# A graph layer on one core: every 32nd quad's rows fetched singly, 32 indices to a register load, a chunk's edge scalars in one transfer

## The chip, the cores and the metric

The kernel runs on one core of one Trainium2 chip. The metric is device microseconds of that core; the time before is the median of three runs, 3920.53 us (3918.47 to 3926.07). A core has five instruction queues that run beside each other and meet at semaphores: TensorE (PE, matrix products), VectorE (DVE), ScalarE (ACT), GpSimd (POOL) and SyncE (SP, which only issues transfers). ACT and POOL issue transfers too.

## What is computed

One message-passing layer over 12,500 nodes with 160 features each (64 scalars and 32 three-vectors) and 400,000 edges that are sorted by destination, then a residual and a layer norm. Cut to what matters:

```
h_s = s @ lin1_ws * a / 8            # node table: 64 scalars
h_v = v @ lin1_wv * a / sqrt(32)     #             and 32 vectors of 3
hid = silu(edge_scalars @ fc_w1 / 8) # 64 scalars an edge
w   = hid @ fc_w2 / 8                # 224 weights an edge: w1..w5
es, ev = h_s[edge_src], h_v[edge_src]
m_s1 = w1 * es * e0                  # messages from weights, gathered rows
m_s2 = w4 * (ev . e1) / 3            # and the edge's four attributes e0, e1
m_v1, m_v2, m_v3 = (w2 * es) e1, w3 * ev * e0, w5 * cross(ev, e1) / 2
agg = segment_sum(messages, edge_dst) / 4
out = layernorm(x + gate(self_connection(x) + lin2(agg)))
```

## The kernel before

**Tables and tiles.** A short first stage writes the node table `h_tab` (12,500 rows of 640 bytes) to device memory. The edges then go in 3125 tiles of 128. Three tiles are a block (`BT`), twelve tiles a side (`SIDE`), two sides a chunk of 24 tiles (`CT`). A step of the main loop (L898) handles a quad: two tiles of each side, so that a chunk is six steps and the loop has 782 of them.

**A step.** `gather` (L468) fetches the quad's 512 rows of `h_tab`: one indirect transfer for each tile, four in all, issued by POOL into one of four buffers `hg`. `weights` (L526) multiplies the hidden layer by `fc_w2` on PE into `pw`. `products` (L538) multiplies `pw` by the gathered rows on DVE into `pr`. `one_hot` and `select_quad` make, on DVE, the matrices by which `add_tile` (L611) sums `pr` into the rows of a block on PE, two steps later (L944). `close` copies a finished pair of blocks out of PSUM (`sa`, ACT, L818); `turned` transposes it on PE and copies it on ACT (`tt`, L625 and L627); `second` applies the output maps on PE (L637) and copies on ACT (`os`, L640); `add` adds it to the accumulator on DVE (L645). `hide` (L776) makes the hidden layer of four tiles of each side at once, two steps ahead: a product of `w1` with the chunk's edge scalars `es` on PE (L463), and a Silu on ACT (L465). The hidden layer, the transposes, the maps and the finishing steps share two PSUM banks (`misc`) in turn. Every 30 steps a piece of the self connection is added, and as destinations are complete, `finish` (L648) norms and stores the nodes.

**Edge scalars.** `load_chunk` (L195) loads a chunk's scalars, in device memory a matrix of 64 rows by 400,000 edges, eight steps ahead (`LEAD`) on SP's queue: the first side to partitions 0 to 63 and the second to 64 to 127, 384 KB each, two transfers. `w1` has `fc_w1` twice on its diagonal, one block for each side. The last, short chunk has sides of three and two tiles.

**Singly fetched quads.** The list `own` (L477) names quads that POOL doesn't gather: every `OWN`-th from step `OWN` + 6, ending four steps before the last. Their rows come as 512 transfers of 640 bytes each, from addresses held in registers. `places` loads the quad's indices as four rows of `at_bytes`, `OWN` + 8 steps ahead; `fetch_rows` (L764) scales them to bytes on DVE, `OWN` + 1 steps ahead, and `rows_of` (L494) cuts them into batches of `BATCH` indices. A batch belongs to SP or to ACT: one instruction loads its indices into registers (L501), and then each of its rows is one transfer (L508) on that queue. `some_rows` (L516) issues the transfers by turns, SP then ACT (`TURNS`); it is called in four places of a step with the counts of `SLOTS`, so the issues stand between the other instructions of both queues. Whatever is left two steps before the quad's own would be an error (L773).

**Order.** The order of each queue is the order of the program (`manual_schedule`). Transfers of SP and ACT take their semaphores from one ring of eight: in the built program an issue waits for the landing of the transfer that used its place before, whichever queue issued that one.

Of the kernel before, what the change touches and what calls it, by code (L numbers as in the profile page):

```python
# [10 lines left out]
F32 = mybir.dt.float32  # L11
# [4 lines left out]
AF = mybir.ActivationFunctionType  # L16
# [5 lines left out]
P = 128  # L22
S = 64
# [11 lines left out]
SIDE = KB * BT  # L35
CT = 2 * SIDE
AHEAD = 3 * CT
NF = 4
OWN = 40
BATCH = 16  # L40
TURNS = "SA"
SLOTS = (4, 3, 4, 3)
LEAD = 8

MARGIN = 128
# [15 lines left out]
def gnn_kernel(  # L61
# [21 lines left out]
    nc = tc.nc  # L83
# [10 lines left out]
    consts = ctx.enter_context(tc.tile_pool(name="consts", bufs=1))  # L94
# [71 lines left out]
    def index(t):  # L166
        a0, idx, _ = ahead(t)
        return idx[:, t - a0:t - a0 + 1]
# [23 lines left out]

    ess = {}

    def load_chunk(c, queue=nc.sync):  # L195
        if c in ess:
            return
        t0, halves = chunks[c]
        es = ess[c] = loads.tile([2 * S, SIDE * P], F32, name="es")
        for half, n in enumerate(halves):  # L200
            to = es[half * S:(half + 1) * S]
            e0 = (t0 + half * halves[0]) * P
            queue.dma_start(to[:, :n * P], es_t[:, e0:e0 + n * P])


    ident = consts.tile([P, P], F32, name="ident")
# [3 lines left out]
    eps = consts.tile([P, 1], F32, name="eps")  # L210
    nc.vector.memset(eps, 1e-5)

    w1 = consts.tile([2 * S, 2 * S], F32, name="w1")
    nc.vector.memset(w1, 0.0)

    w2 = consts.tile([2 * S, 2, NWT], F32, name="w2")
    nc.vector.memset(w2, 0.0)
# [13 lines left out]
    with tc.tile_pool(name="nodes", bufs=len(starts)) as nodes, tc.tile_pool(  # L231
        name="nodes_ps", bufs=6, space=PSUM
# [19 lines left out]
        def spread(w, ap):  # L252

            return bass.AP(tensor=w.tensor, offset=w.offset, ap=[*ap, [1, w.shape[1]]])
# [63 lines left out]
            return m  # L318

        index(0)  # L320
        raw = ends_pool.tile([2 * S, NWT], F32, name="raw")
        for half in range(2):
            r = slice(half * S, (half + 1) * S)
            nc.sync.dma_start(w1[r, r], fc_w1)
            nc.sync.dma_start(raw[r], fc_w2)

        def bases():
# [51 lines left out]
    nc.vector.tensor_scalar_mul(half_at, at, 0.5)  # L379
    iota = consts.tile([P, W], F32, name="iota")  # L380
    nc.vector.tensor_copy(iota, iota_i)
    for half in range(2):
        r = slice(half * S, (half + 1) * S)
        at_c = 0
        for a, b in ((64, 128), (0, 64), (192, 224), (160, 192), (128, 160)):
            nc.vector.tensor_scalar_mul(w2[r, half, at_c:at_c + b - a], raw[r, a:b], 1.0 / math.sqrt(64))
            at_c += b - a
# [66 lines left out]
    def hidden(pool, psum, es, halves, t0, n):  # L454

        ph = psum.tile([2 * S, Q * P], F32, name="ph", tag="misc")
        hid = pool.tile([2 * S, Q * P], F32, name="hid")
        ends = [max(0, min(n, m - t0)) for m in halves]
        assert ends[0] >= ends[1]
        for k, c0, c1 in ((2 * S, 0, ends[1]), (S, ends[1], ends[0])):  # L460
            if c1 > c0:
                c = slice(c0 * P, c1 * P)
                nc.tensor.matmul(ph[:k, c], w1[:k, :k], es[:k, t0 * P + c0 * P:t0 * P + c1 * P],  # L463
                                 start=True, stop=True)
                nc.scalar.activation(hid[:k, c], ph[:k, c], AF.Silu, scale=1.0 / math.sqrt(64))  # L465
        return hid

    def gather(pool, idx):  # L468
# [249 lines left out]
    with tc.tile_pool(  # L718
# [271 lines left out]
        with tc.For_i(0, n_redo, 1):  # L990
# [9 lines left out]
            with tc.For_i(0, n_again, 1) as g, tc.For_i(0, GT, 1) as k:  # L1000
                t = g * GT + k
                idx = loads.tile([P, 1], I32, name="idx1", bufs=1)
                nc.sync.dma_start(idx, src[ds(g, 1), :, ds(k, 1)].rearrange("o p t -> p (o t)"))
                eat = loads.tile([P, 4], F32, name="eat1", bufs=1)
                nc.sync.dma_start(eat, ea[ds(g, 1), :, ds(k, 1)].rearrange("o p t k -> p (o t k)"))
                base0 = loads.tile([P, 1], I32, name="base1", bufs=1)
                nc.sync.dma_start(base0, of_tile[0:1, ds(t, 1)].to_broadcast([P, 1]))
                to = loads.tile([P, 1], I32, name="to1", bufs=1)
                nc.sync.dma_start(to, dst[:, ds(t, 1)])
                line = loads.tile([1, P], I32, name="line1", bufs=1)  # L1010
                with nc.allow_non_contiguous_dma(reason="one tile's destinations"):
                    nc.sync.dma_start(line, dst[:, ds(t, 1)].rearrange("p o -> o p"))
                ends = loads.tile([1, 2], I32, name="ends1", bufs=1)
                for k, op in enumerate((OP.min, OP.max)):
                    nc.vector.tensor_reduce(ends[:, k:k + 1], line, AX.X, op)
                nc.sync.dma_start(least, ends[:, 0:1])
                low = loads.tile([P, 1], I32, name="low1", bufs=1)
                nc.sync.dma_start(low, least.to_broadcast([P, 1]))
                es = loads.tile([2 * S, SIDE * P], F32, name="es")
                nc.sync.dma_start(es[:S, :P], es_t[:, ds(t * P, P)])  # L1020
                hid = hidden(edge, misc_ps, es, (1, 0), 0, 1)
                hg = gather(deep, [idx])
                pr = products(edge, weights(pw_ps, hid, [(0, 0)]), hg, 1)
                r = edge.tile([P, 1], F32, name="r", bufs=1)
                had = edge.tile([P, 2], F32, name="had", bufs=1)
                nc.vector.tensor_tensor(r, to, base0, op=OP.subtract)
                nc.vector.tensor_scalar(had[:, 0:1], r, 0.0, None, op0=OP.is_ge)
                nc.vector.tensor_scalar(had[:, 1:2], r, float(W), float(2 * NP), op0=OP.is_lt,
                                        op1=OP.mult)
                nc.vector.tensor_mul(had[:, 0:1], had[:, 0:1], had[:, 1:2])  # L1030
                nc.vector.tensor_tensor(r, to, low, op=OP.subtract)
                nc.vector.tensor_add(r, r, had[:, 0:1])
                first = nc.values_load(ends[0:1, 0:1], min_val=0, max_val=N - 1)
                last = nc.values_load(ends[0:1, 1:2], min_val=0, max_val=N - 1)
                with tc.For_i(first, last + 1, W) as base:
                    base = nc.s_assert_within(
                        base, 0, N - 1, skip_runtime_bounds_check_because="it is at most `last`")
                    pa = pa_ps.tile([P, 512], F32, name="pa")
                    sel = select(late, r, eat)
                    add_tile(pa, 0, sel, 0, pr[:, 0], start=True, stop=True)  # L1040
                    sa = late.tile([P, NPR], F32, name="sa")
                    nc.scalar.copy(sa[:ROWS], pa[:ROWS, :NPR])
                    tt = late.tile([P, 8, NO, W], F32, name="tt", bufs=1)
                    turned(misc_ps, sa, tt, 0, 1)
                    add(base, second(late, misc_ps, tt, 1), 0)
                    nc.vector.tensor_scalar_add(r, r, -float(W))
# [52 lines left out]
```

## Time and profile before

| | |
|---|---|
| time, median of 3 runs | 3920.53 us (3918.47 to 3926.07) |
| profiled execution: its time, its span | 3915.52 us, 3913.8 us |
| granted TensorE clock, mean | 0.972 |
| PE, matmuls: busy, share | 3634.4 us, 93% |
| DVE | 2441.2 us, 62% |
| ACT | 895.3 us, 23% |
| POOL | 2915.6 us, 74% |
| transfers | 413.16 MB, 106 GB/s over the span |
| single row fetches | 4864 on SP, 4864 on ACT |
| gathers on POOL | 3049 |

The profile is of one execution, taken by the hardware profiler. Busy time counts the work of an engine, not what its sequencer does: transfers that SP or ACT issue, register loads and waits are not in it. In rows of groups, "L472 POOL" is line 472 of the kernel on GpSimd; the names are the tile written, an arrow, and the tiles read; "x3049" is how often; then follow the busy time, the mean duration in ns, the idle time of the engine just before these instructions, and what ended most of it ("issue" is nothing that the profile shows). In rows of waits, "ACT sa L818 <- PE pa L613" is ScalarE idle before line 818 until TensorE's line 613 was done, with us in total, times, and the longest. Rows of the order in time begin with the start and the duration in us. "ACTq" is a queue's own instruction.

### The profile page before, as it was taken

Reading aid. Unit: us, or ns where it says so; the run is one execution under the profiler, and the core shown is the slowest. Engines: PE = TensorE matmul, PEld = TensorE weight load, DVE = VectorE, ACT = ScalarE, POOL = GpSimd, SP = SyncE. Lnnn points to the kernel's source line nnn. Section 1 sums busy time; section 2 is a strip of 40 time slices with the busy share of each in tenths; the row PEclk is TensorE's granted clock in tenths of the full one; section 3 lists DMA queues with packets and bytes.
Section 4 is the critical chain, followed back from the end, with each engine's and each line's share of the span. In section 5 each row is a group of like instructions: output and inputs, shape, how many; then the busy total and the mean of one; then the engine's idle time right before and its main releaser. Section 6 shows DMA issues by size and latency. Waiting matters only on the chain. (4 is left out here: it accounts for less than half of the span.)

```text
span 3913.8 us, 66881 instructions
## 1 busy us (share of the span) xinstructions
PE 3634.4 (93%) x14293; PEld 1589.8 (41%) x14293; DVE 2441.2 (62%) x6532; ACT 895.3 (23%) x2481; POOL 2915.6 (74%) x3096
## 2 busy tenths in 40 slices
PE   6899999999989999899899999989999999989998
PEld 4344344344334444344344343434444344334443
DVE  6656566666655666656566666656666665656655
ACT  2222222222222222222222222222222222222222
POOL 6777777777777777777777777777777777777774
PEclk8999999999999999999999999999999999999999
DMA  7344444444344443443444444444343443444432
GB/s 241 97 104 104 101 105 101 101 105 105 101 105 103 105 108 99 104 109 98 103 106 103 101 109 101 102 103 107 101 111 98 101 112 98 102 103 100 104 99 65
DMA packets 258055, 413.16 MB, mean 106 GB/s; under 512 B 92568, under 2 KB 186273, under 8 KB 257509
## 3 DMA queue, kind: packets, MB, share of 16 engines
q0 software_dynamic: 149312, 260.41, 25.7%
q1 hardware_dynamic: 98004, 145.13, 15.1%
q10 hardware_dynamic: 10322, 3.26, 0.4%
q14 instruction: 302, 2.47, 0.2%
q8 instruction: 115, 1.88, 0.2%
HBM read 392.53 MB, written 16.00 MB: 104 GB/s over the span
## 5 line engine op out<-in xcount | busy, mean ns | idle before, releaser
L472 POOL DMA_INDIRECT hg<-h_tab,idx x3049 | 2885.1, 946 | 942.6 <-issue 834.8
L534 PE MATMUL pw<-w,hid 128*128 128x448 f32 x3126 | 1346.2, 554 | 29.3 <-ACT hid L465 10.8
L613 PE MATMUL pa<-pr,sel 128*64 128x416 f32 x6250 | 1287.4, 533 | 0.2 <-ACT sa L818 0.2
L552 DVE TENSOR_TENSOR pr<-pw,hg 128x384 f32<-128x384 f32 x2289 | 1125.7, 547 | 0.0
L597 DVE TENSOR_TENSOR pw<-rel,iota 128x64 f32<-128x64 int16 x782 | 181.4, 232 | 956.4 <-PE pw L534 953.4
L534 PEld LDWEIGHTS pw<-w,hid 128*128 128x128 f32 x3126 | 553.5, 193 | 487.4 <-issue 420.3
L544 DVE TENSOR_TENSOR pr<-pw,hg 128x512 f32<-128x512 f32 x763 | 527.1, 691 | 346.3 <-DMA hg<-h_tab,idx 250.9
L613 PEld LDWEIGHTS pa<-pr,sel 128*64 128x64 f32 x6250 | 384.4, 138 | 799.0 <-issue 772.9
L818 ACT COPY sa<-pa 128x416 f32<-128x416 f32 x521 | 262.8, 505 | 1081.3 <-DMA hq<-h_tab 612.7
L463 PE MATMUL misc<-es,w 128*128 128x512 f32 (+1 forms) x784 | 446.2, 651 | 20.3 <-DVE rel L425 17.7
L465 ACT ACTIVATE hid<-misc 128x512 f32<-128x512 f32 x392 | 233.5, 596 | 784.0 <-DMA hq<-h_tab 379.3
L622 PEld LDWEIGHTS misc<-ident,sa 128*128 128x128 f32 x2084 | 242.8, 143 | 383.9 <-issue 254.9
L622 PE MATMUL misc<-ident,sa 128*128 128x128 f32 x2084 | 334.1, 284 | 69.2 <-ACT hid L465 56.6
L637 PE MATMUL misc<-tt,l 128*96 128x256 f32 (+5 forms) x1496 | 360.7, 390 | 32.9 <-DVE y L683 26.9
L606 DVE TENSOR_TENSOR sel<-pw,eas 128x256 f32<-128x256 f32 x782 | 324.3, 415 | 9.5 <-ACT eas L580 9.3
L637 PEld LDWEIGHTS misc<-tt,l 128*96 128x96 f32 (+1 forms) x1496 | 233.8, 168 | 179.1 <-issue 98.3
L625 ACT COPY tt<-misc 128x192 f32<-128x192 f32 x521 | 164.6, 316 | 559.8 <-DMA hq<-h_tab 371.4
L463 PEld LDWEIGHTS misc<-es,w 128*128 128x128 f32 x784 | 118.4, 190 | 282.9 <-issue 229.8
L645 DVE TENSOR_TENSOR acc<-acc,os 96x32 f32 x1042 | 195.6, 188 | 25.3 <-ACT os L640 6.8
L627 ACT COPY tt<-misc 128x64 f32<-128x64 f32 x521 | 117.1, 225 | 0.0
L670 PE MATMUL misc<-ident,acc 96*128 96x96 f32 x196 | 35.5, 266 | 77.2 <-DVE pw L597 46.4
L640 ACT COPY os<-misc 96x512 f32<-96x512 f32 (+2 forms) x68 | 38.3, 563 | 208.6 <-PE misc L637 202.3
(89 smaller groups left out, 672.8 us busy)
## 6 DMA issues: line engine op xcount, KB each, us to landing
es<-in_es_t_dram SPq DMA_DIRECT2D x258, 384.0 KB
hq<-h_tab SPq DMA_DIRECT2D x4864, 0.6 KB
hq<-h_tab ACTq DMA_DIRECT2D x4864, 0.6 KB
hg<-h_tab,idx POOLq DMA_INDIRECT x3049
h_tab<-ht POOLq DMA_DIRECT2D x24, 320.0 KB
xt<-in_x_dram SPq DMA_DIRECT2D x23, 320.0 KB
out_dram<-y SPq DMA_DIRECT2D x23, 320.0 KB
xv<-in_xv_t_dram SPq DMA_DIRECT2D x25, 187.5 KB
```

Source lines behind the costliest of these rows:

```text
L463: nc.tensor.matmul(ph[:k, c], w1[:k, :k], es[:k, t0 * P + c0 * P:t0 * P + c1 * P], start=True, stop=True)
L465: nc.scalar.activation(hid[:k, c], ph[:k, c], AF.Silu, scale=1.0 / math.sqrt(64))
L472: nc.gpsimd.indirect_dma_start(out=hg[:, t, :], out_offset=None, in_=h_tab, in_offset=bass.IndirectOffsetOnAxis(ap=i, axis=0))
L534: nc.tensor.matmul(pw[:, t:t + m, :NWT], hid[:m * S, c * P:(c + 1) * P], w2[:m * S, :m], start=True, stop=True)
L544: nc.vector.tensor_mul(two, pw[:, :n, :2 * S].rearrange("p t (k c) -> p t k c", k=2), hg[:, :n, None, :S].to_broadcast([P, n, 2, S]))
L552: nc.vector.tensor_mul(pr[:, :n, first:first + V3].rearrange("p t (i c) -> p t i c", i=3), pw[:, :n, None, 2 * S + k * V:2 * S + (k + 1) * ...
L606: nc.vector.tensor_mul(sel[:, :n], oh[:, :, None, :].to_broadcast([P, n, 4, W]), by_slot(tiles[0][0])[:, u:u + n, :, None].to_broadcast([P ...
L613: nc.tensor.matmul(pa[half * ROWS:(half + 1) * ROWS, :NPR], sel[:, t].rearrange("p k w -> p (k w)"), pr, start=start, stop=stop)
L622: nc.tensor.transpose(pt[:, four * P:four * P + k], sa[:k, c:c + P], ident[:k, :k])
L637: nc.tensor.matmul(po[:, k, :nb], l2[r, terms[to, part, four]], a[:, :nb], start=(n == 0), stop=(n == len(of) - 1))
L645: nc.vector.tensor_add(window, window, os[:, :, b])
L818: nc.scalar.copy(sa, pas.pop(j)[:, :NPR])
```

## The change

Three constants change: `OWN` from 40 to 32, `BATCH` from 16 to 32, `SLOTS` from (4, 3, 4, 3), 14 a step, to (5, 4, 4, 4), 17 a step. `load_chunk` loads a whole chunk by one transfer: row r of side h goes to partition 2 r + h. The short chunk keeps two transfers, to every second partition, after a memset. `w1` follows: `fc_w1` is loaded once with each of its rows on two partitions (`raw1`), and a product on DVE with `halves`, which holds 1/8 on the even or on the odd partitions, makes `w1`. The factor 1/8 before the Silu goes from the activation into `w1`. Lines of the changed kernel stand up to twelve further down.

```diff
@@ -36,10 +36,10 @@
 CT = 2 * SIDE
 AHEAD = 3 * CT
 NF = 4
-OWN = 40
-BATCH = 16
+OWN = 32
+BATCH = 32
 TURNS = "SA"
-SLOTS = (4, 3, 4, 3)
+SLOTS = (5, 4, 4, 4)
 LEAD = 8
 
 MARGIN = 128
@@ -192,15 +192,24 @@
 
     ess = {}
 
+    def side_of(es, half):
+
+        return es.rearrange("(r h) e -> h r e", h=2)[half]
+
     def load_chunk(c, queue=nc.sync):
         if c in ess:
             return
         t0, halves = chunks[c]
         es = ess[c] = loads.tile([2 * S, SIDE * P], F32, name="es")
+        if halves == (SIDE, SIDE):
+            of = es_t[0:1, t0 * P:t0 * P + 1]
+            queue.dma_start(es, bass.AP(tensor=of.tensor, offset=of.offset,
+                                        ap=[[es_t.shape[1], S], [SIDE * P, 2], [1, SIDE * P]]))
+            return
+        nc.vector.memset(es[:, :max(halves) * P], 0.0)
         for half, n in enumerate(halves):
-            to = es[half * S:(half + 1) * S]
             e0 = (t0 + half * halves[0]) * P
-            queue.dma_start(to[:, :n * P], es_t[:, e0:e0 + n * P])
+            queue.dma_start(side_of(es, half)[:, :n * P], es_t[:, e0:e0 + n * P])
 
 
     ident = consts.tile([P, P], F32, name="ident")
@@ -210,8 +219,7 @@
     eps = consts.tile([P, 1], F32, name="eps")
     nc.vector.memset(eps, 1e-5)
 
-    w1 = consts.tile([2 * S, 2 * S], F32, name="w1")
-    nc.vector.memset(w1, 0.0)
+    w1 = consts.tile([2 * S, 2, S], F32, name="w1")
 
     w2 = consts.tile([2 * S, 2, NWT], F32, name="w2")
     nc.vector.memset(w2, 0.0)
@@ -318,10 +326,11 @@
             return m
 
         index(0)
+        raw1 = ends_pool.tile([2 * S, S], F32, name="raw1")
+        nc.sync.dma_start(raw1, spread(fc_w1, [[S, S], [0, 2]]))
         raw = ends_pool.tile([2 * S, NWT], F32, name="raw")
         for half in range(2):
             r = slice(half * S, (half + 1) * S)
-            nc.sync.dma_start(w1[r, r], fc_w1)
             nc.sync.dma_start(raw[r], fc_w2)
 
         def bases():
@@ -379,6 +388,8 @@
     nc.vector.tensor_scalar_mul(half_at, at, 0.5)
     iota = consts.tile([P, W], F32, name="iota")
     nc.vector.tensor_copy(iota, iota_i)
+    nc.vector.tensor_mul(w1, raw1[:, None, :].to_broadcast([2 * S, 2, S]),
+                         halves[:, :, None].to_broadcast([2 * S, 2, S]))
     for half in range(2):
         r = slice(half * S, (half + 1) * S)
         at_c = 0
@@ -460,9 +471,9 @@
         for k, c0, c1 in ((2 * S, 0, ends[1]), (S, ends[1], ends[0])):
             if c1 > c0:
                 c = slice(c0 * P, c1 * P)
-                nc.tensor.matmul(ph[:k, c], w1[:k, :k], es[:k, t0 * P + c0 * P:t0 * P + c1 * P],
-                                 start=True, stop=True)
-                nc.scalar.activation(hid[:k, c], ph[:k, c], AF.Silu, scale=1.0 / math.sqrt(64))
+                nc.tensor.matmul(ph[:k, c], w1.rearrange("p h c -> p (h c)")[:, :k],
+                                 es[:, t0 * P + c0 * P:t0 * P + c1 * P], start=True, stop=True)
+                nc.scalar.activation(hid[:k, c], ph[:k, c], AF.Silu)
         return hid
 
     def gather(pool, idx):
@@ -1017,7 +1028,8 @@
                 low = loads.tile([P, 1], I32, name="low1", bufs=1)
                 nc.sync.dma_start(low, least.to_broadcast([P, 1]))
                 es = loads.tile([2 * S, SIDE * P], F32, name="es")
-                nc.sync.dma_start(es[:S, :P], es_t[:, ds(t * P, P)])
+                nc.vector.memset(es[:, :P], 0.0)
+                nc.sync.dma_start(side_of(es, 0)[:, :P], es_t[:, ds(t * P, P)])
                 hid = hidden(edge, misc_ps, es, (1, 0), 0, 1)
                 hg = gather(deep, [idx])
                 pr = products(edge, weights(pw_ps, hid, [(0, 0)]), hg, 1)
```

## The prediction

> **What bounds the kernel now.** I read the page's first part, then stretches of the span, then the groups of instructions, and last the waits of each engine.
>
> ```profile
> span 3913.8 us, 66881 instructions
> PE 3634.4 (93%) x14293; PEld 1589.8 (41%) x14293; DVE 2441.2 (62%) x6532; ACT 895.3 (23%) x2481; POOL 2915.6 (74%) x3096
> ```
>
> By busy share TensorE would be the bound, with GpSimd (POOL) at 74%. Cut into stretches (columns: length, then busy time and instructions of each engine) it looks otherwise:
>
> ```profile
> 500.00:1000.00 500.00, 468.82 (x1825) 202.85 (x1825) 313.99 (x846) 116.32 (x324) 377.66 (x400) 0.97 0.41 103
> 1000.00:1500.00 500.00, 474.87 (x1850) 204.66 (x1846) 314.61 (x839) 114.22 (x323) 377.77 (x400) 0.98 0.42 104
> ...
> sum 3776.00, PE 3544.36 PEld 1531.12 DVE 2361.77 ACT 862.91 POOL 2850.46; mean PE 393.82 PEld 170.12 DVE 262.42 ACT 95.88 POOL 316.72
> ```
>
> PE's load varies, but POOL issues exactly 400 gathers in each of the two: one per 1.25 us. The sum covers 100 to 3876 us: PE is idle for 3776.0 - 3544.4 = 231.6 us of it.
>
> ```profile
> L472 POOL DMA_INDIRECT hg<-h_tab,idx x3049 | 2885.1, 946 | 942.6 <-issue 834.8 <-DMA hg<-h_tab,idx 26.6 <-DVE pr L552 21.9
> ...
> L544 DVE TENSOR_TENSOR pr<-pw,hg 128x512 f32<-128x512 f32 x762 | 526.9, 691 | 346.3 <-DMA hg<-h_tab,idx 250.9 <-issue 65.6 <-DVE pw L597 9.6
> ```
>
> ```profile
> 51.18 1.05 POOL L472 DMA_INDIRECT hg<-h_tab,idx  x1 [3.44 <-issue]
> ...
> 74.48 0.97 POOL L472 DMA_INDIRECT hg<-h_tab,idx  x1 [3.50 <-DVE l L307]
> ...
> 3874.53 0.94 POOL L472 DMA_INDIRECT hg<-h_tab,idx  x1 [0.30 <-issue]
> ```
>
> A gather is busy for 0.946 us and the next starts 0.30 us later. All 3049 fill 51.18 to 3875.47 us: 3824.3 / 3049 = 1.2543 us each. Of POOL's 942.6 us of idle, 3049 x 0.30 = 914.7 belong to that beat; what is left is 28 us, and without the two waits of the start that the rows show (3.1 and 3.2 over the beat) 21.6 us in the whole run. So POOL never rests, VectorE waits 250.9 us for its gathers, and PE, nearly as loaded, has some 232 us of cushion. The bound is the count of gathers.
>
> **The gathers that go.** A quad of four tiles whose rows are fetched singly costs no gather. Every 40th from step 46, below 778, makes 19 quads; every 32nd from step 38 makes 24. Five quads are 20 gathers: 20 x 1.2543 = 25.1 us off POOL. The built program has these 20 fewer, so that the change does less than it says is excluded. Before the first gather (51.18 us) and after the last (3913.8 - 3875.5 = 38.3 us) almost nothing moves: one transfer issue fewer on POOL and one small product more on VectorE, under 1 us each way.
>
> **What the 24 quads cost.** Each is 512 fetches, half by SP, half by ScalarE (ACT): 24 x 256 = 6144 on each, 1280 more than the 4864. ACT's queue also holds the work that PE waits for.
>
> ```profile
> L508 ACTq DMA_DIRECT2D hq<-h_tab x4864: 234/235/666, 89.5 to 3796.2; - x195
> ```
>
> ```profile
> 2010.58 4.42 ACTq L508 DMA_DIRECT2D hq<-h_tab  x9
> ...
> 2020.07 0.57 ACTq L508 DMA_DIRECT2D hq<-h_tab  x2
> ```
>
> Two unhindered issues take 0.57 us, so one follows another after 0.57 - 0.23 = 0.34 us; the nine took (4.42 - 0.23) / 8 = 0.52, since a fetch first waits for the landing of an earlier one: both queues share a ring of eight semaphores. 1280 x 0.34 = 435 us more ACT time; at 0.52 it would be 666.
>
> Register loads: 16 x 19 = 304 of 16 indices on ACT become 8 x 24 = 192 of 32.
>
> ```profile
> L501 ACTq TENSOR_LOAD <-at_bytes x304: 1185/1297/1877, 88.1 to 3775.0; - x152
> ```
>
> 304 x 1.30 = 395 us now. No load of 32 is in the trace: if the size costs nothing, 192 x 1.30 = 250 (a gain of 145), if it costs twice, 498 (a loss of 103). I take the middle, a gain of 21.
>
> The edge scalars: two transfers a chunk, over 64 partitions each, become one over 128.
>
> ```profile
> L203 SPq DMA_DIRECT2D es<-in_es_t_dram x260: 465/481/1194, 66.8 to 3836.2; - x130
> ```
>
> Those that waited for these transfers (us, times):
>
> ```profile
>   ACT sa L818: 57.7, 16
>   ACT hid L465: 23.1, 11
>   ACT tt L625: 16.7, 6
> ```
>
> SP issues 130 fewer at 0.48 us, 62 us of a queue that has time. ACT's fetches waited 97.5 us behind these transfers; one ring place in two falls away, so between 0 and 49 us of that. I take 25. The first-layer weights in the interleaved order, the scale moved from the activation into them, and one memset for the last chunk leave the counts of matmuls and activations as they are: nothing, behind PE's own work; uncovered, the product and the memset would be two VectorE instructions, under 1 us.
>
> The Trainium skill ("DMA: Bandwidth & Descriptors", Rules for kernel authors) says that transfers to disjoint partition halves serialize, so that one of 128 partitions is to be used. By it the bytes land no sooner and the saved wait lies near my lower end, 0; no row here shows the single transfer.
>
> So ACT gets 435 - 21 - 25 = 389 us more; ends: 435 - 145 - 49 = 241 and 435 + 103 = 538.
>
> **What of it reaches the bound.** ACT's reserve is its waiting for PE:
>
> ```profile
> ACT sa L818 <- PE pa L613: 356.1, 176, 5.7
> ACT hid L465 <- PE misc L463: 305.7, 150, 60.7
> ACT os L640 <- PE misc L637: 202.3, 58, 11.8
> ACT tt L625 <- PE misc L622: 128.5, 78, 9.8
> ...
> ACT g L672 <- PE misc L670: 95.1, 49, 5.3
> ```
>
> Together 1087.7, less the 60.7 of the start: 1027 us. PE in turn waits for ACT:
>
> ```profile
> PE misc L622 <- ACT hid L465: 56.6, 19, 5.2
> ...
> PE misc L798 <- ACT hid L465: 20.9, 26, 3.1
> ...
> PE pw L534 <- ACT hid L465: 10.8, 13, 2.7
> ...
> PE misc L622 <- ACT tt L627: 6.8, 8, 1.4
> ```
>
> That is 95 us. I let it grow as the reserve shrinks, an assumption: 1027 - 389 = 638 gives 95 x 1027 / 638 = 153, 58 more; the ends 241 and 538 give 29 and 105 more. Does a PE stall reach POOL? A stretch in which ACT was blocked:
>
> ```profile
> 2570.00:2610.00 40.00, 35.32 (x135) 14.41 (x135) 25.42 (x71) 6.76 (x19) 30.24 (x33) 0.96 0.41 101
> ```
>
> ```profile
> PE misc L622 <- ACT hid L465: 4.2, 1, 4.2
> ```
>
> PE stalled 4.2 us behind ACT, yet POOL issued 33 gathers in 40 us, its full pace: four buffers of gathered rows take it up. Over the run 21.6 us of POOL waits stand against 95 us of stalls, 0.23 of a us each; so 58 more cost 13 us (29 and 105: 7 and 24).
>
> **The sum.** 25.1 - 13 = 12 us off. The profiled execution took 3915.5 (span 3913.8 and 1.7 around it): 3903.5. The median of the runs, 3920.5, lies 5.0 above it, so I expect 3908. The term ends give 3920.5 - 25.1 + 7 = 3902 and 3920.5 - 25.1 + 24 = 3919; with no passing on at all it is 3895.
>
> **The rivals.**
> - *ACT becomes the pace.* 8.5 issues a step at 0.52 us are 4.4 us, and 8.5 / 32 of a load at 1.3 to 2.6 adds 0.35 to 0.7: 4.8 to 5.1 us, against 3824.3 / 782 = 4.89 us that a step takes now. For it: the nine issues in 4.42 us. Against: the two in 0.57, and the 1027 us that ACT waits for PE. If all 1280 cost 0.52 (666 us, loads and scalars cancelling), the reserve is 361, PE's stalls 95 x 1027 / 361 = 270, that is 175 more. PE's idle time not caused by ACT, 231.6 - 95 = 137 us, is what can be given up; the rest counts: 175 - 137 = 38 us slower than now, 3958. It decides from 137 - 25 = 112 us of further stalls on. The Trainium skill's page "DMA: Bandwidth & Descriptors" (Anatomy of one DMA) puts some 2.0 us of fixed cost on each transfer, and its rules tell to coalesce small ones; on a ring of eight that is 17 x 2.0 / 8 = 4.25 us a step, an estimate near the 4.4 above.
> - *The gain is spent at the quads themselves.* 512 / 17 = 30.1 steps after the start, the last rows leave in the third step ahead of their use; 512 / 14 = 36.6 left them in the fifth. Now that costs nothing:
>
> ```profile
>   DVE pr L544: 1.5, 9
> ```
>
> That is all that VectorE waited for the singly fetched rows. About 1 us at each of 24 quads, passed on, would be 24 us and no change, 3920. Against: two steps are nearly 10 us.
> - *The whole gain.* The stalls don't grow, as the loads and the scalars pay for the fetches: 3895, or 3886 if half of POOL's 21.6 us goes too.
>
> **How the numbers follow.** Forecast 0.40 (3900 to 3916), the whole gain 0.17 (3885 to 3900), no change 0.16 (3913 to 3928), ACT as the pace 0.27 (3928 to 3990). A measurement here tells 0.2%, 7.8 us, from none. Below 3912.7: 0.17 and most of the 0.40, 0.53; above 3928.4: 0.27, and 0.02 of the no-change case, 0.29; between: 0.18. The range 3889 to 3955 leaves out the upper half of the slow case and a sliver of the fast one; the forecast's own is 3900 to 3916.
>
> **What would show it.** Right: 3029 gathers, still one in 1.25 us in the middle, the last ending near 3864 us. ACT's fetches still follow each other after 0.34 us, its waits for PE fall to about 640 us, PE's waits for ACT rise to about 150, POOL's waits over its beat to about 40. A load of 32 near 1.9 us; waits behind the edge scalars under 97. Wrong: fewer than 395 gathers in a 500 us stretch, with VectorE no longer waiting for them and PE for ACT; or VectorE waiting for the singly fetched rows.

## The result, and the profile after

The changed kernel takes 4294.34 us (median of 6 runs, 4278.36 to 4300.62) beside 3921.74 us for the kernel before (6 runs, 3917.51 to 3926.07): a ratio of 1.0948 (95% interval 1.093 to 1.0966). 3908 us were forecast, with 3955 as the upper end; the change costs 373 us.

The page of the profiled execution after (first part, then GpSimd's group; idle time of the engine stands behind the mean of one instruction):

```profile
span 4295.6 us, 71686 instructions
PE 3735.9 (87%) x14293; PEld 1622.4 (38%) x14293; DVE 2461.3 (57%) x6538; ACT 895.1 (21%) x2481; POOL 2894.5 (67%) x3075
...
L483 POOL DMA_INDIRECT hg<-h_tab,idx x3029 | 2864.5, 946 | 1342.8 <-issue 828.0
```

The 20 gathers are gone and one still lasts 946 ns. But POOL's idle time is 1342.8 us; 3029 x 0.30 = 908.7 of it belong to the beat, so 434 us are waits over it, where there were 28. That is 406 us more, and less the 25 us of the 20 gathers 381: the whole difference of the spans (4295.6 - 3913.8 = 382). The loss is GpSimd standing still, so the question is who keeps it waiting.

Stretches of the run after (length; busy time and instructions of PE, PE's weight loads, DVE, ACT, POOL; granted clock):

```profile
500.00:1000.00 500.00, 438.94 (x1645) 186.90 (x1643) 286.21 (x767) 102.50 (x289) 336.62 (x356) 0.94 0.33 94
1000.00:1500.00 500.00, 435.10 (x1658) 186.71 (x1654) 286.12 (x765) 102.19 (x287) 340.20 (x360) 0.95 0.33 94
```

356 and 360 gathers where there were 400: the sign of "wrong" that the prediction named. It is so in every stretch, not at a few places. The waits of all engines after (time, times, longest), the largest first:

```profile
ACT sa L829 <- DMA hq<-h_tab: 989.8, 340, 10.0
...
ACT hid L476 <- DMA hq<-h_tab: 600.8, 258, 11.6
ACT tt L636 <- DMA hq<-h_tab: 461.4, 192, 6.9
POOL hg L483 <- DVE pr L563: 435.2, 182, 9.0
...
ACT sa L829 <- PE pa L624: 216.1, 83, 7.0
...
ACT hid L476 <- PE misc L474: 196.7, 79, 59.8
...
PE misc L633 <- ACT hid L476: 166.6, 57, 10.2
ACT os L651 <- PE misc L648: 142.0, 43, 8.2
...
PE pw L545 <- ACT hid L476: 92.4, 63, 4.3
...
ACT g L683 <- PE misc L681: 68.8, 38, 5.0
...
ACT tt L636 <- PE misc L633: 54.3, 37, 3.1
...
PE misc L809 <- ACT hid L476: 51.0, 33, 4.7
...
PE misc L633 <- ACT tt L638: 16.4, 12, 3.0
```

Read from POOL backwards. POOL waits 435 us for the products `pr` (21.9 before), since a buffer `hg` comes free only with them; the products wait for PE's `pw`; PE waits for `hid` and `tt` of ScalarE; and what `sa`, `hid` and `tt` wait for, 2052 us in the first three rows, are the single fetches ahead of them in ScalarE's own queue. In the profile before these three rows were:

```profile
ACT sa L818 <- DMA hq<-h_tab: 612.7, 244, 7.0
...
ACT hid L465 <- DMA hq<-h_tab: 379.3, 168, 11.2
ACT tt L625 <- DMA hq<-h_tab: 371.4, 162, 7.5
```

1363 us, so 689 more. That is not the price of the 1280 further fetches: a wait stands in the row of whatever ended it last, and e4 below, with not one fetch more than before, has 1608 us in these rows. The four rows of PE waiting for ACT that the prediction summed to 95 us are 326 now; with all such rows it is 110 before and 439 after. One such stall from end to end, in the timeline of the run after (start, length; in brackets the idle time before it and its releaser):

```profile
563.48 0.48 ACT L829 COPY sa<-pa 128x416 f32<-128x416 f32 x1
...
569.48 0.42 SPq L717 DMA_DIRECT2D out_dram<-y  x1
...
569.49 1.62 PE L624 MATMUL pa<-pr,sel 128*64 128x416 f32 x8
...
570.03 4.95 SPq L519 DMA_DIRECT2D hq<-h_tab  x14
...
573.89 5.39 ACTq L519 DMA_DIRECT2D hq<-h_tab  x10
...
579.37 1.28 ACT L476 ACT_TABLE_LOAD   x1 [15.40 <-DMA hq<-h_tab]
...
580.66 0.60 ACT L476 ACTIVATE hid<-misc 128x512 f32<-128x512 f32 x1
...
581.31 1.11 PE L633 MATMUL misc<-ident,sa 128*128 128x128 f32 x4 [10.20 <-ACT hid L476]
...
584.96 0.23 DVE L608 TENSOR_TENSOR pw<-rel,iota 128x64 f32<-128x64 int16 x1 [12.35 <-PE pw L545]
...
587.58 0.94 POOL L483 DMA_INDIRECT hg<-h_tab,idx  x1 [5.96 <-DVE pr L563]
```

ScalarE has copied `sa` at 563.96. Its queue then holds a register load, which ended at 565.6, and ten fetches; the first leaves only at 573.89, as its place in the ring of eight was to be used first by a fetch of SP (which left at 572.07), and SP's queue stood until 569.48 for an output block. The ten take 5.39 us. ACT's next work, behind them, is a table load for `hid`'s Silu, 15.40 us after its last, and `hid` itself starts at 580.66. PE loses 10.2 us, VectorE 12.4; POOL has buffers for part of it and loses 5.96 - 0.30 = 5.7 us. So this stall, one of the longest, has two ingredients, both in ScalarE's queue: the fetches ahead of the work, and their waits for the ring that SP shares.

### The profile page after: what moved, and what is told of

It is laid out like the page before. It is cut to its first block, busy times and chain, and to the rows that moved or that the text cites. A ratio compares the mean times of both kernels' runs of the same rounds, so it can differ in the third digit from the quotient of the medians.

```text
span 4295.6 us, 71686 instructions
## 1 busy us (share of the span) xinstructions
PE 3735.9 (87%) x14293; PEld 1622.4 (38%) x14293; DVE 2461.3 (57%) x6538; ACT 895.1 (21%) x2481; POOL 2894.5 (67%) x3075
## 5 line engine op out<-in xcount | busy, mean ns | idle before, releaser
L483 POOL DMA_INDIRECT hg<-h_tab,idx x3029 | 2864.5, 946 | 1342.8 <-issue 828.0
L545 PE MATMUL pw<-w,hid 128*128 128x448 f32 x3126 | 1394.3, 570 | 93.1 <-ACT hid L476 92.4
L608 DVE TENSOR_TENSOR pw<-rel,iota 128x64 f32<-128x64 int16 x782 | 182.6, 233 | 1420.3 <-PE pw L545 1402.6
L545 PEld LDWEIGHTS pw<-w,hid 128*128 128x128 f32 x3126 | 570.1, 199 | 583.0 <-issue 429.7
L555 DVE TENSOR_TENSOR pr<-pw,hg 128x512 f32<-128x512 f32 x758 | 523.6, 691 | 34.9 <-DMA hg<-h_tab,idx 5.1
L648 PE MATMUL misc<-tt,l 128*96 128x256 f32 (+5 forms) x1496 | 381.0, 406 | 70.2 <-ACT tt L638 40.9
L648 PEld LDWEIGHTS misc<-tt,l 128*96 128x96 f32 (+1 forms) x1496 | 242.9, 175 | 230.5 <-issue 91.6
L687 DVE SCALAR_TENSOR_TENSOR misc<-g,misc 128x64 f32<-128x64 f32 x98 | 22.1, 225 | 180.7 <-ACT g L683 180.4
L810 DVE TENSOR_TENSOR acc<-acc,misc 96x500 f32<-96x500 f32 x50 | 33.5, 671 | 91.3 <-PE misc L809 91.0
```

Of the source, the lines that this page charges most:

```text
L483: nc.gpsimd.indirect_dma_start(out=hg[:, t, :], out_offset=None, in_=h_tab, in_offset=bass.IndirectOffsetOnAxis(ap=i, axis=0))
L545: nc.tensor.matmul(pw[:, t:t + m, :NWT], hid[:m * S, c * P:(c + 1) * P], w2[:m * S, :m], start=True, stop=True)
L555: nc.vector.tensor_mul(two, pw[:, :n, :2 * S].rearrange("p t (k c) -> p t k c", k=2), hg[:, :n, None, :S].to_broadcast([P, n, 2, S]))
L648: nc.tensor.matmul(po[:, k, :nb], l2[r, terms[to, part, four]], a[:, :nb], start=(n == 0), stop=(n == len(of) - 1))
```

## The experiments

On the usual chips the kernel before took 3917 to 3922 us. Two sets of runs fell on chips where it took 5329 and 5333 us; their ratios stand apart, since there GpSimd waits some 1400 us for the products in a kernel as fast as the one before already (last section). "Lost per step" is the time over the kernel before, with 25.1 us added where 20 gathers are gone, divided by the steps in which rows leave (quads x 512 / fetches a step).

| usual chips | fetches a step, quads, load | ratio (95%) | PE waits for ACT, us | POOL waits over its beat, us | lost per step, us |
|---|---|---|---|---|---|
| before | 14, 19, 16 | 1 | 110 | 28 | 0 |
| scalars alone (e1 again) | 14, 19, 16 | 1.0002 (0.9992 to 1.0011) | 153 | 34 | 0.00 |
| load of 32 and scalars (e6) | 14, 19, 32 | 1.0146 (1.0126 to 1.0165) | 207 | 88 | 0.08 |
| fifteen a step (y2 again) | 15, 19, 16 | 1.0259 (1.0233 to 1.0284) | 225 | 134 | 0.15 |
| seventeen, every 40th (e4) | 17, 19, 32 | 1.0628 (1.0609 to 1.0648) | 357 | 278 | 0.43 |
| the change, loads of 16 (y1 again) | 17, 24, 16 | 1.0943 (1.0923 to 1.0963) | 411 | 412 | 0.55 |
| the change | 17, 24, 32 | 1.0948 (1.093 to 1.0966) | 439 | 434 | 0.55 |

**One part at a time.** The edge scalars alone, the load of 32 alone, every 32nd quad alone (all three beside a kernel before of 5329 us), and the scalars once more on a usual chip:

```diff
 # e1, from the changed kernel       # e2, from the kernel before    # e3, from the kernel before
-OWN = 32                            -BATCH = 16                     -OWN = 40
-BATCH = 32                          +BATCH = 32                     -SLOTS = (4, 3, 4, 3)
-SLOTS = (5, 4, 4, 4)                                                +OWN = 32
+OWN = 40                                                            +SLOTS = (5, 4, 4, 4)
+BATCH = 16
+SLOTS = (4, 3, 4, 3)
```

> The changed kernel with the three constants undone (every 40th quad, 14 fetches a step, 16 indices to a load): the edge scalars' single transfer alone. Theory F (ScalarE's single fetches, at about 0.5 us each with their waits, became the pace): nothing of the 374 us is here; 3895 to 3930 us, ScalarE's waits behind the edge scalars well under the 97.5 us of before. Rival E (the single transfer, to every partition with the two sides interleaved, is the slow part): over 4100 us.

> The kernel before with 32 indices to a load and nothing else. Theory F: a load of 32 takes 2.19 us instead of two of 1.30, so 152 on ScalarE are 333 us instead of 395; 3905 to 3940 us. Rival L (a load of 32 holds the queue 2.19 us in one piece, longer than the work behind it can wait, and that is what made ScalarE late): over 4050 us.

> The kernel before with every 32nd quad at 17 fetches a step, with loads of 16 and the two transfers a chunk as before. Theory F: the whole loss is here, and more, since the other two parts no longer help: 4290 to 4400 us, and no more than 365 gathers in a 500 us stretch. Rivals E and L: under 4050 us.

> The single transfer of the edge scalars alone, every 40th quad, 14 a step, loads of 16, on a chip where the kernel before takes about 3920 us. Theory F: ratio 0.990 to 1.000, the transfer's bytes over in about 3 us instead of 4.4. Rival E: over 1.02.

Measured: 1.0018 (0.998 to 1.0055), 0.9975 (0.9947 to 1.0003) and 1.0562 (1.0502 to 1.0621). So on that chip the loss is in the schedule of the single fetches, not in the two other parts; the times in us that were expected don't apply there. On the usual chips e1 gave 1.0002, and the load of 32 does cost something (e6). There the transfer of the scalars is listed with those that waited for it (time, times):

```profile
L206 SPq DMA_DIRECT2D es<-in_es_t_dram x129: 540/555/612, 65.5 to 3814.6; - x129
...
  ACT sa L829: 21.3, 5
  ACT tt L636: 17.9, 7
  ACT hid L476: 9.2, 4
  ACT g L683: 7.1, 2
```

55.5 us of waits; the list of before has 97.5 us in its first three rows and 103.2 in all. But ScalarE did not gain these 48 us: the three rows of waits behind the fetches hold 1452 us in e1 (1363 before). Counted at the ring, from the end of a fetch's register move to its issue, ACT's fetches whose place an edge-scalar transfer had used waited 191 us before (144 fetches) and 191 us in e1 (68 fetches). Half as many had such a place, and on average they waited twice as long.

**Closeness or number.** The change with every 40th quad again, but 17 a step: as many fetches as before, in 30 steps of 40 instead of 37. And 15 a step with loads of 16.

```diff
 # e4, from the changed kernel       # y2, from e1
-OWN = 32                            -SLOTS = (4, 3, 4, 3)
+OWN = 40                            +SLOTS = (4, 3, 4, 4)
```

> The changed kernel with every 40th quad instead of every 32nd; 17 fetches a step stay, so a quad's 512 are out in 30 of 40 steps and ten steps have none. The number of fetches is that of before, their density that of the change. Theory F1 (the density: while 17 a step are issued ScalarE is slower than GpSimd, 5.5 us a step against 4.9, and the ten free steps make little of it up): about 30 of 40 steps at 5.5 us and 10 at 4.7, 782 x 5.3 = 4140 us where the kernel before takes 3920, ratio 1.04 to 1.07. Rival F2 (the number of fetches in the run counts, not how dense they are): ratio 0.99 to 1.01.

> Every 40th quad, loads of 16, the single transfer of the edge scalars, and 15 fetches a step instead of 14 (the last slot 4 instead of 3). The number of fetches is that of the kernel before, only their spacing is closer: 34 steps filled of 40 instead of 37. If the loss grows evenly with the density it is 1.01 to 1.02; if a fetch costs ScalarE 0.34 us and the reserve pays for it, 1.000; if there is a knee above 15, 1.000 to 1.005.

> The same kernel as in the run before (every 40th quad, loads of 16, 15 fetches a step), where it gave 1.0209 beside a kernel before of 5333 us. On the usual chip: 1.01 to 1.02 if the loss grows evenly with the density, 1.000 to 1.005 if there is a knee above 15.

e4 takes 1.0628 with not one fetch more than before: the closeness costs, not the number. Nor is it longer waits for the ring: from the register move to the issue ACT's fetches waited 1011 us in e4 and 973 in e1, 38 us more beside 246 us of loss. y2 gave 1.0209 (1.0158 to 1.026) beside 5333 us and 1.0259 on the usual chip, above all that was expected of it. One more fetch a step, every second of them on ACT, costs 0.15 us in each step in which rows leave; at 17 the 1.5 more on ACT cost 0.43 (e4) and 0.55 us (the change, where the pause between quads is under two steps instead of ten). For each ACT fetch over seven a step that is 0.15 / 0.5 = 0.30, 0.29 and 0.37 us. By these figures ScalarE's queue is about full at 14 a step, and from there on nearly the whole 0.34 us of an issue lands in the step. Among the waits of e4 are the five rows that the prediction took for ScalarE's reserve:

```profile
ACT sa L829 <- PE pa L624: 383.9, 173, 5.8
...
ACT hid L476 <- PE misc L474: 306.0, 142, 60.0
ACT os L651 <- PE misc L648: 169.3, 48, 9.3
ACT tt L636 <- PE misc L633: 169.1, 90, 3.4
...
ACT g L683 <- PE misc L681: 66.7, 46, 2.5
```

Less the 60.0 of the start they sum to 1035 us; before it was 1027. But the sum mixes two kinds of steps: e4 has ten steps of 40 without a fetch, the kernel before three, and in those ScalarE waits some 3 us each for PE. The traces, cut into steps at the instruction of `one_hot` that stands once in each (L597, after the change L608), the first 40 and last 20 left out, show the steps in which ScalarE fetches (means of a step, in us but for the first row):

| steps with fetches | before | fifteen (y2 again) | e4 | the change |
|---|---|---|---|---|
| ScalarE's fetches | 6.9 | 7.5 | 8.7 | 8.6 |
| length of the step | 4.96 | 5.14 | 5.47 | 5.44 |
| ScalarE idle, ended by the fetches ahead | 2.28 | 2.80 | 3.28 | 3.29 |
| ScalarE idle, ended by PE | 1.40 | 1.10 | 1.03 | 0.95 |

From before to the change 1.01 us more goes to the fetches in each such step; 0.45 of it comes out of the waits for PE, and the step grows by 0.48. About half was reserve, and the rest became time although 0.95 us of waiting for PE was left.

**Whose half.** In the changed kernel, SP's half of the fetches left out (x1), then ACT's half (x2); both with `hq` filled with zeros once a quad on VectorE.

```diff
         def batch(t, p0, engine, queue):
+            if queue is nc.sync:      # x2: nc.scalar
+                return [lambda p=p: left.discard((t, p)) for p in range(p0, p0 + BATCH)]
```

> The changed kernel with SyncE's half of the single fetches and their loads left out (their rows stay zero, so the output isn't the reference's); ScalarE issues its 8.5 a step and its loads of 32 as in the change, and the ring of eight semaphores carries half as much. Theory A (ScalarE's own issues and loads are the pace): ratio to the kernel before 1.06 to 1.10. Theory R (ScalarE is late because each of its fetches waits on the ring that it shares with SyncE's): ratio 0.985 to 1.01, and ScalarE's idle time behind the fetches falls from some 2300 us to under 1500.

> The mirror: ScalarE's half of the fetches and its loads are left out (rows stay zero), SyncE issues its 8.5 a step. Theories A and R both: ScalarE is free, GpSimd sets the pace with 3029 gathers, ratio 0.985 to 0.997, which is the 25 us (0.64%) of the prediction's first term. If it is above 1.01, something besides ScalarE's fetches is late, such as SyncE's other loads.

x2: 0.992 (0.9903 to 0.9937), 31 us under its kernel before, PE's waits for ACT 9 us. GpSimd's group there:

```profile
L483 POOL DMA_INDIRECT hg<-h_tab,idx x3029 | 2871.9, 948 | 930.8 <-issue 810.9
```

Its waits over the beat are 930.8 - 908.7 = 22 us. With ScalarE's queue free, GpSimd gives the 25 us of the 20 gathers and a little more. x1: 1.0864 (1.0844 to 1.0884), PE's waits for ACT 435 us, nearly the whole loss with ScalarE's fetches alone. Both fetch the same number of rows, so the traffic as such is not the cause. But x1 changes more than that. Its timeline shows nine fetches in

```profile
2011.35 2.90 ACTq L522 DMA_DIRECT2D hq<-h_tab  x9
```

(2.90 - 0.23) / 8 = 0.334 us each, the unhindered rate; while among the rows of the edge scalars' line

```profile
L206 SPq EVENT_SEMAPHORE  x128: 17/17/32777, 66.8 to 4158.0; - x128
```

SP, with no fetches of its own to pass the time, comes to the next chunk's transfer early and waits up to 32.8 us there for its buffer (at most 27 ns in the change). A fetch of ACT whose ring place that transfer is to use first waits with it. In the trace 126 fetches of x1 waited over 2 us for their place, 616 us together, 394 us of it (76 fetches) for a place of the edge scalars; in the changed kernel it was 125 and 408 us. x1 took short waits away and put long ones in, and ScalarE's waits behind all fetches came to 1927 us, not under the 1500 of theory R. It shows that SP's fetches need not be there, and leaves open how much of the loss is issue and how much is the ring.

**Relief for ScalarE.** The copy `sa` on VectorE, in the changed kernel (x3), with loads of 16 too (y3), and at 14 a step with loads of 16 (z1); the last two beside 5333 us.

```diff
-            nc.scalar.copy(sa, pas.pop(j)[:, :NPR])
+            nc.vector.tensor_copy(sa, pas.pop(j)[:, :NPR])
```

> The changed kernel with the copy of a finished pair of blocks out of PSUM (sa, 521 of 0.505 us) on VectorE instead of ScalarE. If the fetches delay the work that stands behind them in ScalarE's queue, and PE waits for that, then with one such piece of work gone from that queue: ratio 1.03 to 1.08 instead of 1.095. If only the fetches' own rate counts: 1.08 to 1.10.

> The changed kernel with loads of 16 indices, and the copy of the accumulated sums (sa) on VectorE instead of ScalarE. Two reliefs of ScalarE's in-order queue together. If its queue is the cause, they add: the copy on VectorE alone gave 1.0585 against 1.0948, so 1.03 to 1.045 is expected. If something else at 17 a step is the cause (the ring, the transfers themselves), it stays above 1.055.

> Every 40th quad, 14 fetches a step, loads of 16, the single transfer of the edge scalars, and the copy of the accumulated sums on VectorE. If ScalarE's queue already costs the kernel before something (TensorE waits 109 us for it and GpSimd 22 us for the products), the ratio is 0.994 to 0.999. If the kernel before is bound by its gathers alone, 0.999 to 1.001; if VectorE's own order suffers, over 1.001.

x3: 1.0585 (1.0565 to 1.0605); 139 of the 373 us come back for 263 us of copies (521 of 505 ns) taken off ScalarE. That agrees with ScalarE as the pace; the copy's own waits for PE left its queue with it, so the 263 us are not all that was taken off. y3 gave 1.0453 (1.0394 to 1.0511) where y1 gave 1.0476 (1.0425 to 1.0527), which tells nothing apart (1.03 to 1.045 was expected), and z1 0.9996 (0.9969 to 1.0024): at 14 a step the relief buys nothing on that chip. None of these versions beats the kernel before.

**The load of 32.** The change with 14 a step for every 40th quad (e6), and the change with loads of 16 (y1, once beside 5333 us and once on the usual chip).

```diff
 # e6, from the changed kernel       # y1, from the changed kernel
-OWN = 32                            -BATCH = 32
-SLOTS = (5, 4, 4, 4)                +BATCH = 16
+OWN = 40
+SLOTS = (4, 3, 4, 3)
```

> Every 40th quad at 14 a step as before, with the single transfer of the edge scalars and loads of 32: the two other parts of the change together. Both theories: GpSimd stays the pace, ratio 0.994 to 1.003.

> The changed kernel (17 fetches a step for every 32nd quad, single transfer of the edge scalars) with register loads of 16 indices again: 384 loads of 1.30 us on ScalarE instead of 192 of 2.19. If the loss is the density of the fetches and the longer block costs what it cost at 14 a step (about 1.4%), the ratio is 1.07 to 1.08. If the longer block is most of the loss at 17 a step too, it is under 1.04. If the block is nothing at this density, it is 1.09 to 1.10.

> The same kernel as in the run before (the change with register loads of 16 instead of 32), to be compared on a chip where the kernel before takes its usual 3920 us; in the first run it took 5333 us there and the ratio was 1.0476. On the usual chip: 1.07 to 1.08 if the density of the fetches is the loss and the longer block costs what it costs at 14 a step (1.4%); under 1.04 if the longer block is most of the 9.5%; 1.09 to 1.10 if it is nothing here.

e6 came out above what was expected: 1.0146, against 1.0002 with loads of 16. There are half as many loads, but one lasts longer, as their row in e6 shows (shortest, median, longest in ns):

```profile
L512 ACTq TENSOR_LOAD <-at_bytes x152: 2118/2237/2892, 87.2 to 3824.0; - x152
```

152 x 2.24 = 340 us of ScalarE instead of 395, and yet a loss. A block of 2.24 us ahead of `hid` may be worse, where the queue is just full, than two of 1.30 at different times; that is argued, not shown. At 17 a step it is nothing (1.0943 with loads of 16, 1.0948 with 32); there the smaller sum, 192 x 2.19 = 421 against 384 x 1.30 = 499 us, may pay for the longer block. Had e6's 1.4% added to the rest, y1 would have come out at 1.07 to 1.08; it didn't add.

**More on SP.** ACT's share of the fetches cut from a half to 3 in 8, with 17 a step (e5, twice) and with 14 a step for every 40th quad (e7).

```diff
-TURNS = "SA"
+TURNS = "SSASSASA"
```

> The changed kernel, but of every eight fetches ScalarE issues three and SyncE five (6.4 and 10.6 a step instead of 8.5 and 8.5; ScalarE had 7 before). The number of fetches and their rate on the ring of eight semaphores stay. Theory F, ScalarE's own time: its load falls below that of before, GpSimd is the pace again, 3885 to 3925 us. Rival R (the ring of eight, shared by both queues, is what is full: each fetch waits for the landing of one eight places earlier, whoever issues it): ScalarE's wait for each of its fetches grows and the time stays above 4100 us.

> Of every eight fetches ScalarE issues three and SyncE five, on a chip where the kernel before takes about 3920 us (on the first chip, where it took 5329, SyncE's own instructions came 0.7 us apart for stretches, and this kernel had ratio 1.215). Theory F, ScalarE's own time is the pace: ratio 0.99 to 1.01. Rival R, the ring of eight that both queues share, or SyncE: ratio over 1.05.

> Every 40th quad at 14 a step as before, with the single transfer of the edge scalars and loads of 32, and of every eight fetches three on ScalarE and five on SyncE (5.25 and 8.75 a step). Theory F: ScalarE has more reserve than before, GpSimd keeps the pace, and only its waits of some 20 us can go: ratio 0.990 to 1.000. Rival R or SyncE: ratio over 1.02.

Both are far slower: e5 1.215 (1.2076 to 1.2224) beside 5329 us and 1.2735 (1.271 to 1.2759) on the usual chip, e7 1.1103 (1.1083 to 1.1123). The waits of e5 on the usual chip:

```profile
POOL hg L483 <- DVE pr L563: 1033.6, 170, 32.7
ACT sa L829 <- PE pa L624: 838.8, 250, 22.4
...
DVE y L694 <- DMA xt<-in_x_dram: 664.3, 23, 37.8
```

and of e7:

```profile
DVE y L694 <- DMA xt<-in_x_dram: 399.0, 21, 27.2
```

Theory F's 0.99 to 1.01 and 0.990 to 1.000 failed, though ScalarE did come free: PE waits only 96 and 24 us for it. Now ScalarE waits for PE, and VectorE 664 and 399 us for the input rows `xt` that SP loads for the layer norm, up to 37.8 us at a time. SP's queue also carries the loads of every stage, and they come late behind 10.6 fetches a step, and behind 8.75 in e7; in e5 VectorE waits 289 us for the singly fetched rows too. There was no free queue to shift the fetches to.

## Why the prediction was wrong

*GpSimd is the bound, and 20 gathers are 25.1 us.* Right: x2 shows that gain when nothing holds GpSimd up.

*What ScalarE gets: 389 us, at 0.34 us a fetch.* Mis-sized. From one fetch to the next right behind it in ACT's queue the mean was 0.49 us before and 0.47 after (the median 0.33 in both), nearer to the price of the nine hindered ones, which the prediction had beside the other and gave to a rival. The 0.34 is the issue alone; the wait for the ring comes with it, before the change as after it. At 0.47 the 1280 fetches are 602 us, not 435.

*The loads gain 21.* A load of 32 took 2.19 us, near the upper end of 2.59, so they cost 26. By itself that is small; e6 shows that the length of one counts as well.

*The scalars save 25.* Nothing in the time (1.0002), and at the ring nothing in e1 (191 us of waits in both). The rows of those that waited, which the prediction read, fell to 55.5 in e1 and to 13.7 in the change, while the rows of the fetches rose. After the change:

```profile
  ACT tt L636: 10.4, 4
  ACT g L683: 3.3, 1
```

The rule of the Trainium skill that the prediction weighed ("DMA: Bandwidth & Descriptors", Rules for kernel authors), by which two transfers to partition halves serialize and one is to be used, put the saving near 0. The saving was none, but the prediction's reading of the rule, that the bytes land no sooner, does not hold: a chunk's last packet ended 4.4 us after the issue in e1 and 5.7 us after the first of the two issues before (medians). The trace agrees with the rule's advice to use one; the fetches behind it waited as long in all.

*What of it reaches the bound.* Here the prediction failed, in both of its assumptions. The first was that ScalarE's waits for PE, 1027 us in the run, are a reserve that pays for the fetches. The reserve was forecast at 638 us and came out at 618 (the same five rows: 677.9 less the 59.8 of the start), close by luck, for the fetches took more than was forecast and the run grew longer. The stalls came out at 326 instead of 153. In a step with fetches the reserve paid 0.45 of 1.01 us, and 0.95 us of it lay idle while the step grew by 0.48. ScalarE alternates: it waits for PE, then issues its slot of fetches, and only then reaches the work PE waits for; while it waits, it can't issue the fetches that stand behind the wait. The second was that 0.23 of a stall reaches GpSimd. Over the rows of the table from e1 to the change PE's waits for ACT grow by 286 us and POOL's by 400: 1.4 for each. The 0.23 was an average over stalls that the four buffers could take up, such as the prediction's one of 4.2 us; of the 10.2 us shown above they took up 4.5.

Why more than one: PE also got slower. Of the 382 us, 101.5 are the same 14293 matmuls taking 3735.9 instead of 3634.4 us, and 280.3 are PE's idle time (559.7 against 279.4). The clock granted while PE was busy was 0.977 before and 0.954 after: 3634.4 x 0.977 / 0.954 = 3722, so most of it is the granted clock. (The mean over the span also counts the time without work: in e5 it was 0.874, and the same matmuls took 3753 us.) The prediction had no term for it.

*The rivals.* "ACT becomes the pace" was right in naming ScalarE's queue, but short in both of its numbers. Its 4.8 to 5.1 us a step leave out that ScalarE still waits for PE in the step: the steps with fetches took 5.44. At 15 a step its sum is 7.5 x 0.52 + 7.5 / 16 x 1.3 = 4.5 us, under the 4.89, and y2 lost 2.6%. Its price of 38 us was a tenth of the loss, as it let 137 us of PE's idle time be given up first and kept PE's clock. The ring of eight by itself is not full: a fetch that the next user of its place waited for had landed 1.8 us after its issue (median, before and after), and 17 x 1.8 / 8 = 3.8 us a step, an estimate. "The gain is spent at the quads themselves" is out. In the profile after, the products of the 24 quads, at L555, waited for

```profile
  DMA hq<-h_tab: 3.9, 21
```

3.9 us in all. "The whole gain" is what x2 shows without ScalarE's half.

What stays open: the split between the issues of ACT and the ring it shares with SP. Of PE's 95 gaps of over 2 us in the trace after, while rows were fetched, 48 had an ACT fetch waiting over 2 us for its ring place in the 5 us before, 212 of 356 us. But long waits for the ring don't make a loss by themselves: e1, as fast as the kernel before, has 116 of them, 416 us together, where the change has 125 and 408. No kernel with separate rings was tried.

## What to carry to other kernels

An engine that issues transfers and also computes has one order: what it has free is read step by step, apart for steps with and without transfers, and not from its waits summed over the run; and a wait ahead of the transfers in that order is not free time for them. Before making such a queue denser, fill it by one more a step and look at the waits of the engine behind it: 15 instead of 14 here already cost 2.6%. A ratio of stall to loss taken while buffers still absorb is no rate for stalls beyond them.

## What the runs showed of the hardware

**PE's clock after a gap.** Stretches around the stall shown above (columns as before; the clock is the third from the end):

```profile
561.00:571.00 10.00, 10.00 (x41) 3.63 (x39) 9.10 (x30) 1.97 (x3) 7.56 (x9) 1.00 0.32 87
571.00:581.40 10.40, 0.20 (x3) 0.09 (x2) 1.57 (x6) 2.02 (x4) 7.96 (x9) 0.65 0.55 162
581.40:587.00 5.60, 5.60 (x18) 2.68 (x19) 2.01 (x5) 1.12 (x5) 0.23 (x1) 0.74 0.12 20
587.00:593.00 6.00, 6.00 (x24) 2.45 (x24) 4.18 (x14) 1.10 (x2) 4.20 (x5) 1.00 0.17 46
```

After 10 us without work PE runs at 0.74 for the next 5.6 us, just when it should catch up: 18 matmuls, where the next 6.0 us have 24. The Trainium skill says so ("TensorE: Matmul & The Clock Gate", Why this matters for your kernels): a gap of more than some 3 us sends the array back to half rate until it has been busy for about 4. The trace agrees, with a somewhat shorter way back here: the granted clock is 0.5 from 574.06, 2.9 us after the last matmul, to 584.30, 3.0 us after the next. Gaps of over 5 us in it: 5 before, 18 after. In the twelve traces of the usual chips PE's busy time, multiplied by the clock granted in it, lies between 3541 and 3567 us.

**A chip with another bound.** Where the kernel before took 5329 us, the waits of e2, a kernel as fast as it, show

```profile
POOL hg L472 <- DVE pr L552: 1422.5, 315, 14.2
```

and the register moves of ACT's fetches in z1 there

```profile
L519 ACTq MOVE hq<-h_tab x4864: 3/29/1407, 102.3 to 5177.1; - x195
```

One takes up to 1.41 us, 0.038 at most before and after the change on the usual chips. Some instructions of SP's and ACT's sequencers run slower there; why, no run tells. The loss of the closer schedule shows on both kinds of chip, but in other sizes (y1: 1.0476 there, 1.0943 here); that of the load of 32 doesn't show there (e2: 0.9975, e6 here: 1.0146).
